# Four graph layers on one core: layer 1's weight factors transposed into other buffers with their bias sums behind that, and layer 3's statistics queued behind the head's kept values

## The chip, the core and the metric

The kernel runs on one core of a Trainium2 chip. The metric is the device time of one launch in microseconds (us), from the host's data in device memory to the result in device memory. Engines are named as in the profile: PE multiplies matrices (PEld is its loading of weights, which overlaps it), DVE and ACT work on vectors and read PE's results out of PSUM, POOL works on vectors in SBUF only, and SP issues most DMAs. Every engine runs its own queue of instructions in order, and waits on semaphores for the others.

## The reference

An input x of 128 graphs x 64 nodes x 512 features passes through four layers, each x = x + layer(relu(layernorm(x))), all in float32, with one adjacency matrix of 64 x 64 for each graph:

```python
h = maximum(layernorm(x), 0)
# layer 0: a gate from q, k and the adjacency, then a softmax over the 64 nodes
q, k = split(h @ Wqk);  w = mask * sum(q * (adj @ (k * mask)), -1) / sqrt(512)
x = x + softmax(w, axis=1)[:, :, None] * (h @ Wv)
# layer 1: attention whose exponentials are multiplied by adj
query, key, value = h @ Wq.T + bq, h @ Wk.T + bk, h @ Wv.T + bv
weight = adj * exp(query @ key.T);  x = x + (weight / sum(weight, 2)) @ value
# layer 2: attention with 8 heads, scores multiplied by 2 * adj, output projection
# layer 3: H = sum over k = 0..2 of (X_k @ Wk[k] + bk[k]), X_{k+1} = transition @ X_k,
#   with transition from adj * exp(leaky_relu(sj + si + ab)); x = x + relu(H)
```

In layer 1 the product query @ key.T needs Wq and Wk only as one folded matrix, and their biases bq and bk only as a column u, a row c and a number d.

## The kernel before

**Blocks and layers.** The 8192 tokens are cut into 32 blocks of 256 (two tiles of 128 tokens). Layers 0 and 1 alternate over pairs of blocks (`steps`), and write x to device memory; then layer 2 runs over the 32 blocks, then layer 3 (`layer3_step`).

**A product.** Each product of 256 tokens with a 512 x 512 weight is made with seven block products instead of eight (class `Product`): weights carry precomputed differences (`formed`, `chore`, in the places T1 to T4 of a weight slot), and the tokens carry four sums S made on POOL (`sums`). A product holds two PSUM banks, ab and dc. Its early block products (1, 6 into ab, 5, 4 into dc) are read by `keep_ab` (ACT copies a to p1, DVE adds b + p1 into u2, line 287) and `keep_dc` before the late ones (2, 7 into ab, 3 into dc) add to the same banks. `store` (lines 308 to 312) then writes the result with one copy on ACT, three additions on DVE and one on POOL. The pool `ps_mm` has four banks, so two products are under way at a time. `side_by_side` issues the early parts of two products, then their late parts, and calls the actions of `between` in between.

**Statistics.** `norm` makes the mean and variance of a block on DVE (lines 170 to 173), the power -1/2 on POOL (L175, rstd), a product on DVE (L177, nmr), and h on ACT (L185). `transposed` then turns h on PE (L196) into hT, copied by DVE and ACT.

**Weight factors.** For layers 0 and 1 the two factors q and k are loaded in a weight slot each (`factor`), transposed on PE (`transpose_weights`, L429), copied back over themselves (L435 on ACT, L437 on DVE), and multiplied (`folded`, L449) into the folded weight m. A slot has room for seven pieces of 512 columns; a factor takes four.

**Layer 1's set-up** (`setup1`) is a generator whose parts are issued by `next(setup)` between the parts of the work of layer 0: the loads; then five sums on DVE for d and u (`dots`, L487); then four more for c with a trip through device memory that spreads the row c1 over all partitions (L500, L502); then transposes, folding and the formed differences. Each of the sums multiplies 128 x 512 elements and adds them up; the bias lies in memory in the order (p k), and the factor is read in that order too, with a stride. The actions `further` call `next(setup)` twice during the first block of layer 0. Within `folded`, the end of block 0's softmax (`layer0_end`, its matmul sm_w at L406) is called after the first of four groups of matmuls.

**A layer 3 step** for block b makes y2 and y1 side by side (the head, `layer3_head`), then y0 (the tail). Between its early parts, `begin` makes the statistics and h of block b + 2; between early and late parts stands the end of block b - 1 (`layer3_end`: po on PE, tz on ACT at L934, an addition on POOL at L936, an addition into x on DVE at L937, the store). `layer3_dots` (L834) follows the tail.

**Order.** The instructions are put into the engines' queues by a planner (the tile framework's scheduler). It goes by data dependencies, by the program's order as a priority, and by when its own cost model believes an instruction to be ready; work from far down the program can be issued early. `tc.issue_after(ins)` says that what the block traces on the engine of `ins` is queued behind `ins`. It is an order of issue on that one engine, not a wait.

Of the kernel before, what the change touches and what calls it, by code (L numbers as in the profile page):

```python
# [8 lines left out]
FP = mybir.dt.float32  # L9
AF = mybir.ActivationFunctionType  # L10
ALU = mybir.AluOpType
AX = mybir.AxisListType

P = 128
N = 64
D = 512
K = D // P
# [8 lines left out]
def kernel(ctx: ExitStack, tc: tile.TileContext, a: dict, out: bass.AP):  # L26
# [7 lines left out]
    nc = tc.nc  # L34
# [4 lines left out]
    const = ctx.enter_context(tc.tile_pool(name="const", bufs=1))  # L39
    wpool = ctx.enter_context(tc.tile_pool(name="weights", bufs=1))  # L40
    big = ctx.enter_context(tc.tile_pool(name="big", bufs=2))
    med = ctx.enter_context(tc.tile_pool(name="med", bufs=3))
    snap = ctx.enter_context(tc.tile_pool(name="snap", bufs=2))
    small = ctx.enter_context(tc.tile_pool(name="small", bufs=3))
    ps_tr = ctx.enter_context(tc.tile_pool(name="ps_tr", bufs=2, space=bass.MemoryType.PSUM))
# [34 lines left out]
    def slot(place: int, name: str):  # L80
        return wpool.tile([P, 7, 2, F], FP, tag=f"w{place}", name=name)
# [3 lines left out]
    def formed(w, engine):  # L85
        for to, x, y in sums_of_weights:
            last = engine.tensor_tensor(w[:, to], w[:, x], w[:, y], ALU.subtract)  # L87
        return last
# [39 lines left out]

    def factor(ap, which: str, layer: int, queue):

        w = slot({"q": 4, "k": 5}[which], f"{which}_{layer}")
        w = w.rearrange("p s k o -> p (s k o)")[:, : K * D].rearrange("p (k o) -> p k o", k=K)
        for k in range(K):
            queue.dma_start(w[:, k, :], ap[k * P : (k + 1) * P, :])
        return w

    f0 = [
# [66 lines left out]
    def norm_T(x, name: str):  # L204
        hs = norm(x, name)
        return hs, transposed(hs, name)

    behind = [None]

    def sums(hT, name: str, places=("S", "S")):  # L210
# [18 lines left out]
    class Product:  # L229
# [52 lines left out]
        def keep_ab(self):  # L282


            self.p1, self.u2 = self.temp("p1"), self.temp("u2")
            nc.scalar.copy(self.p1, self.a)  # L286
            self.kept = nc.vector.tensor_tensor(self.u2, self.b, self.p1, ALU.add)  # L287

        def keep_dc(self, bias=None):

# [126 lines left out]
    def transpose_weights(*pairs):  # L417

        pts = [
            [  # L420
                pool.tile([P, K, P], FP, tag=tag, name=f"tw_{name}_{m}")
                for m, (pool, tag) in enumerate(places)
            ]
            for w, name, places, on_scalar in pairs
        ]
        for k in range(K):
            for (w, *_), mine in zip(pairs, pts):
                for m, pt in enumerate(mine):
                    nc.tensor.transpose(pt[:, k, :], w[:, k, m * P : (m + 1) * P], ident)  # L429
        last = [None, None]  # L430
        for m in range(K):
            for (w, _, _, on_scalar), mine in zip(pairs, pts):
                flat = mine[m].rearrange("p k i -> p (k i)")
                if m in on_scalar:
                    last[1] = nc.scalar.copy(w[:, m, :], flat)  # L435
                else:
                    last[0] = nc.vector.tensor_copy(w[:, m, :], flat)  # L437
        return last

    in_mm = ((ps_mm, "mm"),) * K  # L440
    elsewhere = ((ps_tr, "tr"), (ps_sc, "sc")) * 2

    def folded(aT, bT, layer: int, place: int, amid=lambda: None):

        m = slot(place, f"fold{layer}")
        for i in range(K):
            pm = ps_mm.tile([P, D], FP, tag="mm", name=f"pf_{layer}_{i}")
            for k in range(K):
                nc.tensor.matmul(  # L449
                    pm, aT[:, k, i * P : (i + 1) * P], bT[:, k, :],  # L450
                    start=(k == 0), stop=(k == K - 1),
                )
            nc.scalar.copy(m[:, quarters[i // 2][0], i % 2, :], pm[:, :F])
            nc.vector.tensor_copy(m[:, quarters[i // 2][1], i % 2, :], pm[:, F:])
            if i == 1 - layer:
                amid()
        return m

    def setup0():
        m = folded(*f0, 0, 0, lambda: turned(0))  # L460
        last = formed(m, nc.vector)

        msc = const.tile([P, n_tok // P], FP, tag="msc", name="msc")
        with tc.issue_after(behind_norm[0][1].ins):
            nc.vector.tensor_scalar(msc, mcol, -(float(D) ** -0.5), None, ALU.mult)
        return m, msc, last

    def setup1():


        qT, kT = (factor(a[f"L1_W{c}"], c, 1, nc.sync) for c in "qk")

        bias = big.tile([P, 2, P, K], FP, tag="v", name="b1qk")
        for i, n in enumerate(("L1_bq", "L1_bk")):
            nc.sync.dma_start(
                bias[:, i], a[n].rearrange("(o p) k -> o p k", o=1).to_broadcast([P, P, K])
            )
        w1v = fetched("L1_Wv", 3, nc.sync)
        yield
        u = const.tile([P, K], FP, tag="u1", name="u1")  # L480
        cc = small.tile([P, K], FP, tag="cc", name="c1", bufs=1)
        d = const.tile([P, 1], FP, tag="d1", name="d1")

        def dots(*sums):
            for to, x, by in sums:
                junk = med.tile([P, P, K], FP, tag="e2", name="bias1", bufs=3)
                nc.vector.scalar_tensor_tensor(  # L487
                    junk, x, 1.0, bias[:, by], ALU.mult, ALU.mult, accum_out=to
                )

        def columns(w):
            return [w[:, k, :].rearrange("q (k p) -> q p k", k=K) for k in range(K)]

        dots((d, bias[:, 0], 1))
        dots(*((u[:, k : k + 1], x, 1) for k, x in enumerate(columns(qT))))
        yield
        dots(*((cc[:, k : k + 1], x, 0) for k, x in enumerate(columns(kT))))

        crow = tc.dram_tile([1, D], FP, name="c1_row")
        nc.sync.dma_start(crow.rearrange("o (k p) -> p (o k)", p=P), cc)  # L500
        c1 = const.tile([P, 2, D + 1], FP, tag="u3", name="c1")[:, 0, :D]
        nc.sync.dma_start(c1, crow.to_broadcast([P, D]))  # L502
        yield
        transpose_weights((qT, "q1", in_mm, range(K)))
        transpose_weights((kT, "k1", elsewhere, (1, 3)))
        m = folded(kT, qT, 1, 2, lambda: layer0_end(0, *softmax))
        formed(m, nc.gpsimd)
        with tc.issue_after(behind[0].ins):
            formed(w1v, nc.gpsimd)
        w2 = [fetched(f"L2_W{c}", 4 + i, nc.sync) for i, c in enumerate("qk")]  # L510
        for w in w2:
            later(w)
        yield m, u, c1, d, w1v, w2
# [471 lines left out]
    def turned(i: int):  # L985
        layer, b = steps[i]
        normed[i] = normed[i], transposed(normed[i], f"{layer}_{b}")
# [19 lines left out]
    def turned2(b: int):  # L1007
# [1 line left out]
            normed2[b] = transposed(normed2[b], f"2_{b}")  # L1009

    taken = transpose_weights(
        (f0[0], "q0", in_mm, (2, 3)),
        (f0[1], "k0", ((ps_sc, "sc"), (ps_tr, "tr")) * 2, (0, 1)),
    )
    with tc.issue_after(taken[0].ins), tc.issue_after(taken[1].ins):
        prepare(0)
# [12 lines left out]
    for i, (layer, b) in enumerate(steps):  # L1029
        if i == len(steps) - 2:  # L1030
            fetch2(0)
        between = [[], [chore], []]
        if i == 0:
            for n in (1, 2):
                between[n].append(further)
        if i == 1:
            begun = []
            made1 = next(setup)
        for n, end in begun:
            between[n].append(end)  # L1040
        begun = []
        if i + 1 < len(steps):
            between[0].append(lambda: prepare(i + 1) if i else second())
            between[2].append(lambda: turned(i + 1))
        else:
            fetch2(1)
            between[0].append(lambda: first2(0, of_v))
            between[2].append(lambda: turned2(0))
        if layer == 0:
            softmax = layer0(b, *loaded[b], *normed[i], between, open_end if b % 2 else nothing)  # L1050
            begun = [(0, lambda b=b, softmax=softmax: layer0_end(b, *softmax))]
        else:
            of_v, *attention = layer1(
                b, *loaded[b], *normed[i], between, open_end if b % 2 else nothing
            )

            def open_end(b=b, a=attention):
                layer1_end(b, loaded[b][0], *a, x1[b])
                if b == n_blk - 2:
                    fetch2(2)  # L1060

        if i == len(steps) - 3:
            made2 = setup2()
# [2 lines left out]
    w3, made_in = {}, []  # L1066
    made3 = normed3 = None

    ending, behind_y0 = [lambda: None], [None]

    def layer3_step(b: int, ahead: bool = True):

# [6 lines left out]
        def begin():  # L1079
            nonlocal normed3  # L1080
            if b + 2 < n_blk and ahead:
                with tc.issue_after(behind_y0[0].ins):
                    normed3 = layer3_norm(b + 2)

        y = layer3_head(b, ops, [
            [begin], [ending.pop()], [lambda: next(stages, None), lambda: next(stages, None)]
        ])
        yield
        tail = layer3_tail(b, al, ops, y)
# [2 lines left out]
            yield  # L1092
        r, y0, kept = next(tail)
        ending.append(lambda: layer3_end(b, x, al, y, r, y0))
        behind_y0[0] = kept
        if b + 1 == n_blk:
            ending[0] = lambda: layer3_last(b, x, al, y, r, y0, ops, kept)
        if b + 2 < n_blk:
# [146 lines left out]
```

## Time and profile before

| | |
|---|---|
| Time before, median of 3 runs | 2640.34 us (2638.94 to 2640.64) |
| The profiled execution's own time | 2638.83 us |
| Span of the profiled execution, first to last instruction | 2637.0 us |
| Granted TensorE clock | 1.000 |
| Weight factors of layer 0, folding, first statistics | 0 to 26 us |
| Layer 0, block 0, and layer 1's set-up | 26 to 64 us |
| Layers 0 and 1, four steps for a pair of blocks | 59.7 us |
| Layer 2, one block | 28.63 us |
| Layer 3, one block, from b = 2 to b = 28 | 21.93 us |

The page gives the busy time of each engine, the chain of work that ended last, the costliest groups of instructions and the DMA issues. Line numbers (L257) are those of the kernel before. A line of a timeline reads: start, duration, engine, line, operation, output <- inputs, shapes, how many, and in brackets the idle time of the engine before it with what ended it. Equal instructions that follow each other are merged: x4 with 1.03 us is four of them from the first start to the last end. A matmul with a 4-byte type is recorded twice per call. A matmul's end is modelled, so what PE lost is read from the distance of starts. A line of waits reads: engine, what waited <- what it waited for, us in total, how often, and the longest.

### The profile page before, as it was taken

What the parts mean: (1) busy time and instruction counts of PE and PEld (TensorE: products, weight loads), DVE (VectorE), ACT (ScalarE), POOL (GpSimd) and SP (SyncE); (2) the same over time, 40 slices, a digit from 0 to 9 for tenths busy, and PEclk for the clock granted to TensorE, in tenths of its full rate; (3) what the DMA queues carried; (4) which work ended last, traced back from release to release, by engine and by line L of the source; (5) the groups of instructions that cost most, each with busy time, mean ns of one, the idle gap of its engine ahead of it and who ended that gap; (6) DMA issues with size and microseconds to landing.
All of it is one profiled execution on the core that took longest, in us unless ns stands there. A gap on an engine that the chain in (4) does not pass through costs nothing.

```text
span 2637.0 us, 52785 instructions
## 1 busy us (share of the span) xinstructions
PE 2618.7 (99%) x20752; PEld 2253.1 (85%) x20752; DVE 1701.5 (65%) x4400; ACT 939.9 (36%) x2292; POOL 1289.4 (49%) x1582
## 2 busy tenths in 40 slices
PE   8999999999999999999999999999999999999999
PEld 5888888888888889999999999999887777777777
DVE  5666666666666666566556656656666666666665
ACT  2343434333443343333333333333323333333332
POOL 2443343333334345656655655655565555555554
PEclk9999999999999999999999999999999999999999
DMA  5111111111111122111111111111211111111110
GB/s 162 62 40 35 35 35 36 35 46 41 38 48 35 35 67 79 45 45 40 45 46 40 37 53 37 39 53 38 74 51 52 52 52 51 52 52 52 51 51 33
DMA packets 103200, 129.81 MB, mean 49 GB/s; under 512 B 40870, under 2 KB 50086, under 8 KB 102952
## 3 DMA queue, kind: packets, MB, share of 16 engines
q1 hardware_dynamic: 102376, 125.38, 14.4%
q8 instruction: 164, 2.69, 0.4%
q10 hardware_dynamic: 576, 1.05, 0.1%
q14 instruction: 84, 0.69, 0.1%
HBM read 76.07 MB, written 50.34 MB: 48 GB/s over the span
## 4 chain that ended last, share of the span: by engine, by line
PE 95%; DVE 2%; DMA 1%; POOL 1%; ACT 0%; issue 0%; SPq 0%; POOLq 0%; ACTq 0%; DVEq 0%
PE ab_v L257 12%; PE ab_y L257 12%; PE dc_v L257 9%; PE dc_y L257 9%; PE ab_g L250 4%; PE ab_k L250 4%; PE ab_q L250 4%; PE tr L196 4%; PE ab_g L257 4%; PE ab_o L257 4%; PE dc_g L250 3%; PE po L398 3%; PE dc_g L257 3%; PE dc_k L250 3%; PE dc_q L250 3%; PE dc_o L257 3%
## 5 line engine op out<-in xcount | busy, mean ns | idle before, releaser
L175 POOL TENSOR_TENSOR rstd<-ve,neghalf 128x2 f32<-128x2 f32 x128 | 89.6, 700 | 445.2 <-DVE ve L173 445.1
L185 ACT ACTIVATE h<-x,nmr,rstd 128x512 f32<-128x512 f32 x256 | 194.4, 806 | 212.6 <-DVE nmr L177 212.6
L257 PE MATMUL ab_y<-L_Wk,hT 128*128 128x256 f32 x768 | 206.9, 392 | 0.6 <-DVE u_y L309 0.3
L257 PE MATMUL ab_v<-L_Wv,hT 128*128 128x256 f32 x768 | 200.9, 384 | 1.6 <-DVE u_v L287 0.9
L257 PEld LDWEIGHTS ab_y<-L_Wk,hT 128*128 128x128 f32 x768 | 135.7, 189 | 74.1 <-DVE r L896 23.5
L257 PE MATMUL dc_v<-L_Wv,S 128*128 128x256 f32 x768 | 197.3, 379 | 0.0
L257 PE MATMUL ab_y<-L_Wk,S 128*128 128x256 f32 x768 | 197.1, 379 | 0.0
L257 PE MATMUL ab_v<-L_Wv,S 128*128 128x256 f32 x768 | 197.1, 379 | 0.0
L257 PE MATMUL dc_y<-L_Wk,S 128*128 128x256 f32 x768 | 192.8, 380 | 0.0
L170 DVE BATCH_NORM_STATS2 stats<-x 128x6 f32<-128x512 f32 x256 | 164.9, 674 | 8.3 <-DMA x<-x 8.3
L257 PEld LDWEIGHTS dc_y<-L_Wk,S 128*128 128x128 f32 x768 | 145.6, 190 | 20.9 <-issue 0.8
L257 PEld LDWEIGHTS ab_y<-L_Wk,S 128*128 128x128 f32 x768 | 145.9, 190 | 19.8
L257 PEld LDWEIGHTS ab_v<-L_Wv,S 128*128 128x128 f32 x768 | 145.9, 190 | 19.8
L257 PEld LDWEIGHTS dc_v<-L_Wv,S 128*128 128x128 f32 x768 | 143.4, 190 | 18.9 <-POOL L_Wv L87 0.8
L257 PEld LDWEIGHTS ab_v<-L_Wv,hT 128*128 128x128 f32 x768 | 135.8, 190 | 17.6 <-DVE u_v L287 1.3
L936 POOL TENSOR_TENSOR tz<-tz,y 128x512 f32<-128x512 f32 x62 | 90.1, 1453 | 105.6 <-ACT tz L934 105.5
L196 PE MATMUL tr<-ident,h 128*128 128x128 f32 x1024 | 133.3, 273 | 0.0
L196 PEld LDWEIGHTS tr<-ident,h 128*128 128x128 f32 x1024 | 117.8, 141 | 7.7 <-issue 0.5
L222 POOL TENSOR_TENSOR S<-hT 128x256 f32<-128x256 f32 x128 | 100.6, 786 | 43.8 <-ACT hT L199 43.6
L225 POOL TENSOR_TENSOR S<-hT 128x256 f32<-128x256 f32 x128 | 106.9, 835 | 7.4 <-DVE hT L201 7.3
L223 POOL TENSOR_TENSOR S<-S,hT 128x256 f32<-128x256 f32 x128 | 101.9, 796 | 11.4 <-DVE ve L173 9.4
L286 ACT COPY p_y<-ab_y 128x256 f32<-128x256 f32 x96 | 35.1, 366 | 200.6 <-PE ab_y L257 192.0
(250 smaller groups left out, 6407.7 us busy)
## 6 DMA issues: line engine op xcount, KB each, us to landing
x<-x SPq DMA_DIRECT2D x128, 512.0 KB, 3.5
x<-in_x_dram SPq DMA_DIRECT2D x32, 512.0 KB, 3.5
out_dram<-x SPq DMA_DIRECT2D x31, 512.0 KB, 2.8
adjT<-in_adjT_dram SPq DMA_DIRECT2D x64, 64.0 KB, 2.0
adjq<-in_adj_dram SPq DMA_DIRECT2D x64, 64.0 KB, 2.3
L_Wk<-in_L_Wk_dram SPq DMA_DIRECT2D x16, 256.0 KB, 4.5
L_Wv<-in_L_Wv_dram SPq DMA_DIRECT2D x12, 256.0 KB, 5.2
q<-in_L_Wqk_dram ACTq DMA_DIRECT2D x4, 256.0 KB, 4.7
```

The source lines that it names most:

```text
L170: nc.vector.bn_stats(stats[:, t, :], x[:, t, :])
L175: by_rows = nc.gpsimd.tensor_tensor(rstd, ve, neghalf, ALU.pow)
L185: nc.scalar.activation(h, x[:, t, :], AF.Relu, bias=nmr[:, t : t + 1], scale=rstd[:, t : t + 1])
L196: nc.tensor.transpose(pt[:, k, :], h[:, k * P : (k + 1) * P], ident)
L222: nc.gpsimd.tensor_tensor(S1, A21, A22, ALU.add)
L223: nc.gpsimd.tensor_tensor(S2, S1, A11, ALU.subtract)
L225: behind[0] = nc.gpsimd.tensor_tensor(S3, A11, A21, ALU.subtract)
L250: nc.tensor.matmul(dst[:, m * P : (m + 1) * P], w[:, place, k, m * P : (m + 1) * P], left[:, k, :], start=key not in self.begun, stop=last ...
L257: nc.tensor.matmul(dst, left[:, k, :], w[:, place, k, :], start=key not in self.begun, stop=last and k == 1, skip_group_check=True,)
L286: nc.scalar.copy(self.p1, self.a)
L398: nc.tensor.matmul(ps[t][half[g ^ t]], e[half[g], t, :], us[t][half[g]], start=True, stop=True)
L936: nc.gpsimd.tensor_tensor(tz[t], tz[t], y0[:, t, :], ALU.add)
```

## The change

`factor` returns seven pieces of a slot, of which the first four are loaded. In layer 1 the transposed factors are written to the three free pieces of the own slot and to one place (T1 or T2) of the folded weight's slot, not over the loaded ones. The loaded ones stay, and so the nine bias sums are made after the transposing: on DVE behind the last copy of k, with the bias rows rearranged by two ACT copies beforehand, so that bias and factor are both read in a row. The end of block 0's softmax is put on PE behind the first group of folding matmuls. In layer 3 `begin` moves from the head's first place to its second and is queued on DVE behind the latest `keep_ab` sum, not behind the last addition of the preceding y0. The parts of it that matter:

```diff
     def factor(ap, which: str, layer: int, queue):
-        w = slot({"q": 4, "k": 5}[which], f"{which}_{layer}")
-        w = w.rearrange("p s k o -> p (s k o)")[:, : K * D].rearrange("p (k o) -> p k o", k=K)
+        w = slot({"q": 4, "k": 5}[which], f"{which}_{layer}").rearrange("p s k o -> p (s k o)")
+        w = [w[:, k * D : (k + 1) * D] for k in range(7)]
         for k in range(K):
-            queue.dma_start(w[:, k, :], ap[k * P : (k + 1) * P, :])
+            queue.dma_start(w[k], ap[k * P : (k + 1) * P, :])
         return w
...
             self.kept = nc.vector.tensor_tensor(self.u2, self.b, self.p1, ALU.add)
+            kept_ab[0] = self.kept
...
-            for (w, _, _, on_scalar), mine in zip(pairs, pts):
+            for (_, _, _, on_scalar, to), mine in zip(pairs, pts):
                 flat = mine[m].rearrange("p k i -> p (k i)")
                 if m in on_scalar:
-                    last[1] = nc.scalar.copy(w[:, m, :], flat)
+                    last[1] = nc.scalar.copy(to[m], flat)
                 else:
-                    last[0] = nc.vector.tensor_copy(w[:, m, :], flat)
+                    last[0] = nc.vector.tensor_copy(to[m], flat)
...
             if i == 1 - layer:
-                amid()
+                with tc.issue_after(last.ins):
+                    amid()
...
         w1v = fetched("L1_Wv", 3, nc.sync)
         yield
+
+        rows = [med.tile([P, K, P], FP, tag="pT", name=f"b1_{i}", bufs=3) for i in range(2)]
+        for i, r in enumerate(rows):
+            nc.scalar.copy(r.rearrange("o k p -> o p k"), bias[:, i])
+        rows = [r.rearrange("o k p -> o (k p)") for r in rows]
+        yield
...
-        dots((d, bias[:, 0], 1))
-        dots(*((u[:, k : k + 1], x, 1) for k, x in enumerate(columns(qT))))
-        yield
-        dots(*((cc[:, k : k + 1], x, 0) for k, x in enumerate(columns(kT))))
-
-        crow = tc.dram_tile([1, D], FP, name="c1_row")
-        nc.sync.dma_start(crow.rearrange("o (k p) -> p (o k)", p=P), cc)
         c1 = const.tile([P, 2, D + 1], FP, tag="u3", name="c1")[:, 0, :D]
-        nc.sync.dma_start(c1, crow.to_broadcast([P, D]))
-        yield
-        transpose_weights((qT, "q1", in_mm, range(K)))
-        transpose_weights((kT, "k1", elsewhere, (1, 3)))
-        m = folded(kT, qT, 1, 2, lambda: layer0_end(0, *softmax))
+        m = slot(2, "fold1")
+        qt, kt = (
+            f[K:] + [m[:, spare].rearrange("p k o -> p (k o)")]
+            for f, spare in ((qT, T1), (kT, T2))
+        )
+        transpose_weights((qT, "q1", in_mm, range(K), qt))
+        taken = transpose_weights((kT, "k1", elsewhere, (1, 3), kt))
+        folded(kt, qt, 1, m, lambda: layer0_end(0, *softmax))
         formed(m, nc.gpsimd)
         with tc.issue_after(behind[0].ins):
             formed(w1v, nc.gpsimd)
+
+        def dots(*sums):
+            for to, x, by in sums:
+                junk = med.tile([P, D], FP, tag="e2", name="bias1", bufs=3)
+                nc.vector.scalar_tensor_tensor(
+                    junk, x, 1.0, rows[by], ALU.mult, ALU.mult, accum_out=to
+                )
+
+        with tc.issue_after(taken[0].ins):
+            dots((d, rows[0], 1))
+            dots(*((u[:, k : k + 1], qT[k], 1) for k in range(K)))
+            dots(*((cc[:, k : k + 1], kT[k], 0) for k in range(K)))
+
+        crow = tc.dram_tile([1, D], FP, name="c1_row")
+        nc.sync.dma_start(crow.rearrange("o (k p) -> p (o k)", p=P), cc)
+        nc.sync.dma_start(c1, crow.to_broadcast([P, D]))
...
         if i == 0:
-            for n in (1, 2):
-                between[n].append(further)
+            between[1].append(further)
...
             if b + 2 < n_blk and ahead:
-                with tc.issue_after(behind_y0[0].ins):
+                with tc.issue_after(kept_ab[0].ins):
                     normed3 = layer3_norm(b + 2)
         y = layer3_head(b, ops, [
-            [begin], [ending.pop()], [lambda: next(stages, None), lambda: next(stages, None)]
+            [], [begin, ending.pop()], [lambda: next(stages, None), lambda: next(stages, None)]
         ])
```

Layer 0's factors are still transposed over themselves.

More of the change, by code (lines that the diff above doesn't have):

```diff
@@ L206, in norm_T @@
         return hs, transposed(hs, name)
+    kept_ab = [None]
     behind = [None]
@@ L423, in transpose_weights @@
             ]
-            for w, name, places, on_scalar in pairs
+            for w, name, places, on_scalar, to in pairs
         ]
@@ L428, in transpose_weights @@
                 for m, pt in enumerate(mine):
-                    nc.tensor.transpose(pt[:, k, :], w[:, k, m * P : (m + 1) * P], ident)
+                    nc.tensor.transpose(pt[:, k, :], w[k][:, m * P : (m + 1) * P], ident)
         last = [None, None]
         for m in range(K):
-            for (w, _, _, on_scalar), mine in zip(pairs, pts):
+            for (_, _, _, on_scalar, to), mine in zip(pairs, pts):
                 flat = mine[m].rearrange("p k i -> p (k i)")
                 if m in on_scalar:
-                    last[1] = nc.scalar.copy(w[:, m, :], flat)
+                    last[1] = nc.scalar.copy(to[m], flat)
                 else:
-                    last[0] = nc.vector.tensor_copy(w[:, m, :], flat)
+                    last[0] = nc.vector.tensor_copy(to[m], flat)
         return last
@@ L441, with folded @@
     elsewhere = ((ps_tr, "tr"), (ps_sc, "sc")) * 2
-    def folded(aT, bT, layer: int, place: int, amid=lambda: None):
-        m = slot(place, f"fold{layer}")
+    def folded(aT, bT, layer: int, m, amid=lambda: None):
         for i in range(K):
@@ L448, in folded @@
             for k in range(K):
-                nc.tensor.matmul(
-                    pm, aT[:, k, i * P : (i + 1) * P], bT[:, k, :],
+                last = nc.tensor.matmul(
+                    pm, aT[k][:, i * P : (i + 1) * P], bT[k],
                     start=(k == 0), stop=(k == K - 1),
@@ L455, in folded @@
             if i == 1 - layer:
-                amid()
+                with tc.issue_after(last.ins):
+                    amid()
         return m
     def setup0():
-        m = folded(*f0, 0, 0, lambda: turned(0))
+        m = folded(*f0, 0, slot(0, "fold0"), lambda: turned(0))
         last = formed(m, nc.vector)
@@ L482, in setup1 @@
         d = const.tile([P, 1], FP, tag="d1", name="d1")
[L484 to L492, printed above, removed]
-        dots((d, bias[:, 0], 1))
-        dots(*((u[:, k : k + 1], x, 1) for k, x in enumerate(columns(qT))))
-        yield
-        dots(*((cc[:, k : k + 1], x, 0) for k, x in enumerate(columns(kT))))
-        crow = tc.dram_tile([1, D], FP, name="c1_row")
-        nc.sync.dma_start(crow.rearrange("o (k p) -> p (o k)", p=P), cc)
-        c1 = const.tile([P, 2, D + 1], FP, tag="u3", name="c1")[:, 0, :D]
-        nc.sync.dma_start(c1, crow.to_broadcast([P, D]))
-        yield
-        transpose_weights((qT, "q1", in_mm, range(K)))
-        transpose_weights((kT, "k1", elsewhere, (1, 3)))
-        m = folded(kT, qT, 1, 2, lambda: layer0_end(0, *softmax))
+        c1 = const.tile([P, 2, D + 1], FP, tag="u3", name="c1")[:, 0, :D]
+        m = slot(2, "fold1")
[6 more added lines that the diff above has]
+        folded(kt, qt, 1, m, lambda: layer0_end(0, *softmax))
         formed(m, nc.gpsimd)
@@ L1011 @@
     taken = transpose_weights(
-        (f0[0], "q0", in_mm, (2, 3)),
-        (f0[1], "k0", ((ps_sc, "sc"), (ps_tr, "tr")) * 2, (0, 1)),
+        (f0[0], "q0", in_mm, (2, 3), f0[0]),
+        (f0[1], "k0", ((ps_sc, "sc"), (ps_tr, "tr")) * 2, (0, 1), f0[1]),
     )
@@ L1067 @@
     made3 = normed3 = None
-    ending, behind_y0 = [lambda: None], [None]
+    ending = [lambda: None]
     def layer3_step(b: int, ahead: bool = True):
@@ L1094, in layer3_step @@
         ending.append(lambda: layer3_end(b, x, al, y, r, y0))
-        behind_y0[0] = kept
         if b + 1 == n_blk:
```

## The prediction

> **What bounds it now.** The page first, for the busy shares; then the waits of PE, for what is left to win.
>
> ```profile
> PE 2618.7 (99%) x20752; PEld 2253.1 (85%) x20752; DVE 1701.5 (65%) x4400; ACT 939.9 (36%) x2292; POOL 1289.4 (49%) x1582
> ```
> ```profile
> PE ab_g L257 <- DVE u_g L287: 2.1, 1, 2.1
> PE sm_w L406 <- DVE wd L555: 1.0, 1, 1.0
> PE ab_v L257 <- DVE u_v L287: 0.9, 1, 0.9
> PE pf L449 <- DVE q L437: 0.6, 1, 0.6
> PE tw_q L429 <- DVE u_g L309: 0.6, 1, 0.6
> ```
>
> PE is the bound; only what it loses between matmuls can be won. Apart from 4.8 us for the first weights and a tail of 5.5 us (last matmul 2631.5, span 2637.0) these are among its longest waits. All but the fourth lie at 35 to 50 us, where layer 1 is set up. The timeline there:
>
> ```profile
> 33.49 1.03 PE L257 MATMUL dc_g<-fold,hT 128*128 128x256 f32 x4
> 33.87 1.04 DVE L487 SCALAR_TENSOR_TENSOR bias<-q,b1qk 128x512 f32<-128x512 f32 x1 [1.72 <-DMA q<-in_L_Wq_dram]
> 34.92 0.41 DVE L287 TENSOR_TENSOR u_v<-ab_v,p_v 128x256 f32<-128x256 f32 x1
> 35.39 1.13 PE L257 MATMUL ab_v<-L_Wv,hT 128*128 128x256 f32 x4 [0.87 <-DVE u_v L287]
> 40.79 0.41 DVE L287 TENSOR_TENSOR u_g<-ab_g,p_g 128x256 f32<-128x256 f32 x1
> 41.26 1.13 PE L257 MATMUL ab_g<-fold,hT 128*128 128x256 f32 x4 [2.14 <-DVE u_g L287]
> 47.00 1.91 PE L429 MATMUL tw_k<-ident,k 128*128 128x128 f32 x16
> 49.87 0.46 PE L406 MATMUL sm_w<-wd,ones_bd 128*128 128x128 f32 x2 [0.96 <-DVE wd L555]
> 50.38 1.13 PE L449 MATMUL pf<-q,k 128*128 128x512 f32 x2
> ```
>
> The small sums u_v and u_g, which release PE, stand in DVE's queue behind the bias sums (L487).
>
> Layer 3 hides a second loss. 27 steps take 21.93 us, but the step that makes no statistics (b = 30) takes 21.78. Two timelines, a step with and the step without:
>
> ```profile
> 2244.26 1.52 ACT L185 ACTIVATE h<-x,nmr,rstd 128x512 f32<-128x512 f32 x2 [3.40 <-DVE nmr L177]
> 2246.20 2.10 ACT L934 ACTIVATE tz<-po,r 128x512 f32<-128x512 f32 x3
> 2250.12 0.69 DVE L937 SCALAR_TENSOR_TENSOR x<-tz,x 128x512 f32<-128x512 f32 x1 [1.16 <-POOL tz L936]
> 2250.30 1.03 PE L257 MATMUL dc_y<-L_Wk,S 128*128 128x256 f32 x4
> 2250.73 0.42 DVE L309 TENSOR_TENSOR u_y<-ab_y,p_y 128x256 f32<-128x256 f32 x1
> 2251.21 1.13 PE L257 MATMUL ab_y<-L_Wk,hT 128*128 128x256 f32 x4
> 2252.18 1.03 PE L257 MATMUL ab_y<-L_Wk,S 128*128 128x256 f32 x4
> ```
> ```profile
> 2600.32 0.42 DVE L309 TENSOR_TENSOR u_y<-ab_y,p_y 128x256 f32<-128x256 f32 x1
> 2601.20 1.03 PE L257 MATMUL dc_y<-L_Wk,S 128*128 128x256 f32 x4
> 2602.07 1.03 PE L257 MATMUL ab_y<-L_Wk,hT 128*128 128x256 f32 x4
> ```
>
> A group of four matmuls costs 0.864. With statistics, y0's first group starts 0.91 after the one before it, 0.06 after L309's end (L309 frees its PSUM bank), and lasts 0.97: 0.15 lost. Without, it starts 0.87 after, and L309 had ended 1.33 earlier. The chain: statistics, rstd, nmr, h on ACT, tz behind h, POOL's add L936, L937, L309.
>
> **Setup, part by part.** From dc_g at 33.49 to pf at 50.38 are 16.89 us. PE's work in it: seven groups of four (6.05), 8 transposes at 0.109 (0.87), 32 weight transposes (3.49), sm_w (0.22): 10.63. So 6.26 are lost.
>
> *Nine sums behind the copies of k.* Without them u_v can run at about 31.5 (p_v ends 30.60, statistics of block 1 31.39) and is needed at 34.35. Those statistics give h about 2.5 us earlier than 37.5, and u_g follows p_g (ab_g ends 33.5) by 36, needed at 37.8. The stores that free the banks for tw_q are no longer held up either, except dc_g's: its adds L310 and L311 end some 0.9 after the last late group, but 12 of tw_q's 16 transposes (1.31) need other banks. I charge 0.2; 0 to 0.6.
>
> *Transposing into other buffers.* As many copies as before (q 4 on ACT, k 2 and 2), none free: pf still waits for them. The nearest row is layer 0's same sequence, transposes, copies, pf: "PE pf <- DVE q", 0.6, and 0.8 counted between starts. Charge 0.8. That wd comes earlier than the copies needs POOL's store of gv (0.73) before its four S sums; if it comes after them, agg and wd still end near 43.5, and k is transposed at about 44.
>
> *sm_w behind the first pf group*: the same 0.22, inside pf; its consumers (x, then layer 1's h at 56.65, transposed at 74.72) keep some 10 us.
>
> So 6.26 - 0.8 - 0.2 = 5.26; I take 5.1, ends 4.0 and 5.5.
>
> *What the sums cost where they go.* Contiguous they should take the 0.65 of the bias by bias row, not 1.04: nine, 6 us on DVE during pf (13.7 us), which uses DVE for 4 copies of 0.42 and layer 0's softmax. Done by about 54. Hidden by pf; behind them on DVE wait block 0's statistics (53.68 now), with 10 us to spare. SP: c_row's DMA moves from 43.17 to about 54, lands 8.0 later as now, then c1; its reader (L601, 86.94) becomes 82. Behind c1 on SP wait L2's first weights, from 59.4 to about 62.4; their first chore (L100) could stand in POOL's queue until 67, and the next POOL work there (L312) comes at 70. If that cover went, PE would lose what is over.
>
> *fold's T1 and T2 hold q's and k's last quarter*, so the first of POOL's four subtractions (58.96 now) waits for pf's end: four at 1.24 to about 65; first reader 78.18 - 5.1 = 73.
>
> *Two row copies on ACT*, writing successive elements 512 bytes apart; no row shows that. Bounds: 0.59 (ACT's contiguous copy, L199) and 1.06 (DVE reading with such a stride, L487). ACT is idle from 20.14 to 22.99 for both; nothing binds them to a place, see the rivals.
>
> **Layer 3.** The statistics (2 x 0.64, 2 x 0.17, 0.17), rstd 0.70, nmr 0.16 and h 1.52 are all moved, no DMA. They now follow y1's kept sum, which follows p_y (possible at 2243.0, ACT idle): kept 2243.7, ve 2245.5, rstd 2246.3, h from 2246.6. tz can start when po lands, 2244.9, instead of 2246.20, so L937 and L309 come earlier by up to 1.3. POOL's rstd may stand before an L936 (+0.7 of L309's 1.33 in hand), still early enough. h's next reader, the dots at 2259.93, has 11 us. So 27 x 0.153 = 4.1, and step 2, which loses 0.58 at the same place: 4.7; ends 0 and 4.7 here, and below nothing in a rival. Step 1's statistics wait for a DMA and stay.
>
> The Trainium skill, Perfetto Trace Analysis, section Optimization Strategy, says that a gap that repeats can mean too few buffers. This gap does wait for a PSUM bank, and the change adds none: by the rule alone layer 3 would bring 0 and the sum would be 5.1. The step without statistics has the same banks and no gap, so the row decides.
>
> **Sum.** 5.1 + 4.7 = 9.8; I take 9.7. Span 2637.0 - 9.7 = 2627.3; its own time 2638.83 becomes 2629.1. That execution was 1.5 below the median, 2640.34, so 2630.6.
>
> **Rivals.**
> 1. *Layer 3's wait stays* (h slips between the parts of tz, 1.5 us in front of the last, more than the 1.33 in hand). For: ACT's order is the planner's, and h and tz's last part are ready within half a microsecond. Against: then L309 is ready before L937 and may go first. Where the loss stays as it is, setup alone remains: 2640.3 - 5.1 = 2635.2. With all of h in front, L309 ends 1.52 - 1.33 + 0.06 = 0.25 late, a step loses 0.35 instead of 0.15, and 27 x 0.2 = 5.4 eats the setup: 2640.6.
> 2. *A wait in setup takes the removed one's place*: the row copies stand before block 0's h (15.67) and wait for b1qk, issued at 12.43 and 13.18 while neighbours land in 4.5 to 7 us. h at 20 to 22, the transposes at 18.48 lose 2.5 to 4.5: 2633 to 2635. Against: h is ready before they land.
> 3. *Slower*: in layer 3 rstd stands on POOL behind both tz additions, and ACT's h still in front of y2's copy (L308). Then L936 ends at 2248.6, rstd 2249.3, h 2249.5 to 2251.1, L308 2251.45, L309 2251.9: PE at 2251.95, not 2251.21, 0.74 a step. 27 x 0.74 = 20 less 5.1: 2655. It decides from 0.19 a step on, where it eats the setup's gain. Against: a planner that puts rstd so late sees h late too, and L308 first.
> 4. *It does not do what it says*: the statistics already come after y1's kept sum. Step 2242 denies it (statistics 2241.3, kept 2246.07).
>
> **Chances.** Forecast 0.68; rival 1, 0.12; rival 2, 0.10; rival 3, 0.09; rival 4, 0.01. A measurement of this kernel can tell about 0.2%, 5.3 us, from no change. Faster by more: forecast, a third of rival 1, two thirds of rival 2, 0.78; slower 0.09; within, 0.13. The range runs from 2629.0 (setup 5.5, layer 3 4.7, 1 us of spread between runs) to 2636.5 (rival 1's first case with setup at 4.0); beyond it lie the rest of rival 1 and rival 3.
>
> **What would show it.** Right: L487's successors after the k copies; no wait of ab_v or ab_g in 30 to 45; pf about 5 us earlier; layer 3's steps 21.78, L309 ended 0.5 us or more before y0's first group. Wrong: pf later than 46.5; steps of 21.9 or more; new PE waits on h, S or tr.

## The result, and the profile after

The changed kernel takes 2663.52 us, the median of 5 runs, beside 2639.22 us for the kernel before on the same chip: a ratio of 1.0092, 95% interval 1.0077 to 1.0106. It is 24.3 us slower. The profiled execution is the slowest of the five, 2664.91 us; its span is 2663.1 us, 26.1 longer than the span before.

The waits of PE first (engine, line and tile waited for; us in total, times, longest):

```profile
PE dc_y L258 <- DVE y L313: 13.2, 28, 0.7
...
PE tr L196 <- ACT h L185: 3.6, 1, 3.6
PE pf L450 <- ACT k L437: 1.2, 2, 0.6
```

u_v and u_g of the set-up are gone from the head of the list, as forecast. Two waits are new: one of 3.6 us for block 0's h, and one of about 0.46 us (once 0.75) in 28 of layer 3's steps. Three of the prediction's signs of being wrong are there: a new wait of PE for h, steps above 21.9, and pf later than 46.5.

**The start.** ScalarE's timeline of the changed kernel (start, duration, engine, line, operation; in brackets the idle time before and what ended it), then TensorE's:

```profile
19.19 1.94 ACT L485 COPY b<-b1qk 128x512 f32<-128x512 f32 x2 [7.23 <-DMA b1qk<-in_L_bq_dram]
20.94 1.50 ACT L185 ACTIVATE h<-x,nmr,rstd 128x512 f32<-128x512 f32 x2
```
```profile
21.79 1.97 PE L196 MATMUL tr<-ident,h 128*128 128x128 f32 x8 [3.62 <-ACT h L185]
23.55 9.16 PE L450 MATMUL pf<-k,q 128*128 128x512 f32 x16
...
51.13 2.38 PE L450 MATMUL pf<-q,k 128*128 128x512 f32 x5 [0.59 <-ACT k L437]
```

The two row copies stand in ScalarE's queue in front of block 0's h, which ran at 15.67 before. They wait for b1qk until 19.19, h starts at 20.94, and the transposes at 21.79 instead of 18.48. That is rival 2. What comes next was in no case of the prediction: the eight transposes take 1.97 us and sixteen matmuls of pf 9.16, where the same sixteen took 7.03 before. The windows view gives the reason (window, length, PE busy and matmuls, granted clock as a share of full speed, DMA share, GB/s):

```profile
22.00:24.00 2.00, 2.00 (x9) 0.50 1.08 346
...
28.00:30.00 2.00, 2.00 (x6) 1.00 0.24 45
```

At the end of the idle time the clock was 0.50, and it came back to 1.00 before 28. So the matmuls at 32 us, 26.32 before, start 6.32 late: 3.3 from the wait and 3.0 from the clock. From there to layer 1's pf the change wins what it was forecast to win: pf at 51.13 against 50.38 is only 0.75 late, so 5.57 us came back.

**Layer 3.** 27 steps take 22.82 us each (one of them 23.11), 21.93 before; the step without statistics is 21.78 in both. One step of the changed kernel:

```profile
2256.41 0.69 ACT L943 ACTIVATE tz<-po,r 128x512 f32<-128x512 f32 x1 [0.59 <-PE po L400]
...
2257.76 1.27 POOL L945 TENSOR_TENSOR tz<-tz,y 128x512 f32<-128x512 f32 x1
2257.83 1.22 DVE L177 SCALAR_TENSOR_TENSOR nmr<-mv,rstd 128x2 f32<-128x2 f32 x1 [0.81 <-POOL rstd L175]
...
2259.08 1.52 ACT L185 ACTIVATE h<-x,nmr,rstd 128x512 f32<-128x512 f32 x2 [1.99 <-DVE nmr L177]
...
2260.61 1.38 ACT L943 ACTIVATE tz<-po,r 64x512 f32<-64x512 f32 x2
...
2261.82 1.03 PE L258 MATMUL dc_y<-L_Wk,S 128*128 128x256 f32 x4
2262.02 0.37 ACT L310 COPY y<-ab_y 128x256 f32<-128x256 f32 x1
...
2262.42 0.42 DVE L311 TENSOR_TENSOR u_y<-ab_y,p_y 128x256 f32<-128x256 f32 x1 [2.46 <-ACT y L310]
...
2262.90 1.13 PE L258 MATMUL ab_y<-L_Wk,hT 128*128 128x256 f32 x4
...
2263.44 1.20 DVE L946 SCALAR_TENSOR_TENSOR x<-tz,x 128x512 f32<-128x512 f32 x1 [0.59 <-POOL tz L945]
...
2263.87 1.03 PE L258 MATMUL ab_y<-L_Wk,S 128*128 128x256 f32 x4
...
2264.90 0.41 DVE L313 TENSOR_TENSOR y<-dc_y,u_y 128x256 f32<-128x256 f32 x1
...
2265.36 1.13 PE L258 MATMUL dc_y<-L_Wk,S 128*128 128x256 f32 x4 [0.46 <-DVE y L313]
...
2266.33 1.03 PE L258 MATMUL dc_y<-L_Wk,hT 128*128 128x256 f32 x4
```

Read it from the top. tz's first part runs as soon as po lands. Then ScalarE idles for 1.99 us, since next in its queue is h, and h waits for nmr: an instruction on 128x2 numbers that takes 1.22 us here, ending with POOL's addition that started 0.07 before it (it takes 0.16 where POOL is quiet). Only at 2260.61, behind h, come tz's other two parts, 3.5 us after the first one ended. Everything behind is late: y2's copy L310, then u_y (L311), which releases y0's ab group; then L946, 1.20 us beside POOL's next work, in front of L312 and L313, which release the dc group. From dc_y at 2261.82 to the second ab group at 2263.87 are 2.05 us, where two groups need 1.73: 0.32 lost. From there to 2266.33 are 2.46: another 0.73. Together 1.05 on 21.78, which makes the 22.82 of a step. Against before it is 27 x 0.89 = 24.0.

### The profile page after: what moved, and what is told of

Its sections match the earlier page's. It is cut to its first block, busy times and chain, and to the rows that moved or that the text cites. A ratio compares the mean times of both kernels' runs of the same rounds, so it can differ in the third digit from the quotient of the medians.

```text
span 2663.1 us, 52838 instructions
## 1 busy us (share of the span) xinstructions
PE 2630.5 (99%) x20752; PEld 2251.0 (85%) x20752; DVE 1739.0 (65%) x4400; ACT 949.1 (36%) x2294; POOL 1287.8 (48%) x1582
## 3 DMA queue, kind: packets, MB, share of 16 engines
q10 hardware_dynamic: 576, 1.05, 0.1%
## 4 chain that ended last, share of the span: by engine, by line
PE 84%; DVE 6%; ACT 4%; POOL 3%; issue 2%; DMA 1%; ACTq 0%; POOLq 0%; DVEq 0%
PE ab_v L258 12%; PE dc_v L258 9%; PE ab_y L258 7%; PE dc_y L258 7%; PE ab_g L251 4%; PE ab_k L251 4%; PE ab_q L251 4%; PE ab_g L258 4%; PE ab_o L258 4%; PE dc_g L251 3%; PE tr L196 3%; PE dc_g L258 3%; PE dc_k L251 3%; PE dc_q L251 3%; PE dc_o L258 3%; PE po L400 2%
## 5 line engine op out<-in xcount | busy, mean ns | idle before, releaser
L223 POOL TENSOR_TENSOR S<-hT 128x256 f32<-128x256 f32 x128 | 113.5, 886 | 46.8 <-ACT hT L199 46.5
L177 DVE SCALAR_TENSOR_TENSOR nmr<-mv,rstd 128x2 f32<-128x2 f32 x128 | 59.6, 466 | 109.9 <-POOL rstd L175 109.9
L945 POOL TENSOR_TENSOR tz<-tz,y 128x512 f32<-128x512 f32 x62 | 79.4, 1280 | 104.9 <-ACT tz L943 101.3
```

The lines of the kernel that those rows point to most:

```text
L177: scaled = nc.vector.scalar_tensor_tensor(nmr, mv[:, :, 0], -1.0, rstd, ALU.mult, ALU.mult)
L223: nc.gpsimd.tensor_tensor(S1, A21, A22, ALU.add)
L945: nc.gpsimd.tensor_tensor(tz[t], tz[t], y0[:, t, :], ALU.add)
```

## The experiments

Theory A, formed from this trace: the two losses are separate. At the start it is the place of the row copies, in front of block 0's h; in layer 3 it is h between the parts of tz, late because nmr runs beside POOL. Twelve kernels follow, all timed against the kernel before.

### Each part alone

e2_stats_back is the changed kernel with layer 3's statistics back where they were; e3_stats_alone is the kernel before with only layer 3's edit made. The lines of e2, which e3's turn round:

```
-                with tc.issue_after(kept_ab[0].ins):
+                with tc.issue_after(behind_y0[0].ins):
-            [], [begin, ending.pop()], [lambda: ...
+            [begin], [ending.pop()], [lambda: ...
```

> The changed kernel with layer 3's edit undone: the statistics are made in their old place behind y0's kept sum; the set-up as changed. Theory A (the steps' 22.82 us come from the place of the statistics alone): steps back to 21.93 us, 27 x 0.89 = 24 us less, about 2639.5 us. Rival theory B (the set-up's new buffers shift what the planner does in layer 3): steps stay near 22.8 us, about 2663 us.

> The kernel before with layer 3's edit alone. Theory A: steps of 22.82 instead of 21.93 us, 2640.3 + 24 to 24.6 = about 2664.5 us. Rival theory B (it takes both parts to slow layer 3): steps near 21.8 to 21.9 us, 2636 to 2640 us.

Measured: e2 2637.29 us, ratio 0.9994 (0.9985 to 1.0004), steps of 21.93, some 2 us less than forecast; e3 2663.16 us, 1.0091 (1.0076 to 1.0106), steps of 22.8. Layer 3's edit by itself costs the whole 24 us, and the set-up has no share in it. Theory B falls.

e2's trace also bears on the clock. Its pf starts at 47.28, 3.85 earlier than the changed kernel's. The counterparts of the lines above:

```profile
20.63 1.36 PE L196 MATMUL tr<-ident,h 128*128 128x128 f32 x8 [2.08 <-ACT h L185]
```
```profile
22.00:24.00 2.00, 2.00 (x6) 1.00 1.11 329
```

b1qk landed 1.2 earlier here, PE idled 2.08 us, and the clock stayed at 1.00. In b3 below the same wait was 3.47 us, and the clock was 0.50 from 22 to 24. The Trainium skill, TensorE: Matmul & The Clock Gate, section "HAM oscillation — how this bites in real kernels", gives about 3.4 us of idle time as the point from which the clock falls. These three rows, 2.08 on one side, 3.47 and 3.62 on the other, agree. e3's timeline and window, with the old set-up, do not:

```profile
41.02 1.90 PE L258 MATMUL ab_g<-fold,hT 128*128 128x256 f32 x4 [2.15 <-DVE u_g L288]
```
```profile
42.00:44.00 2.00, 2.00 (x7) 0.50 0.06 0
```

The clock fell here after 2.15 us, and so it did in f5 below, behind the same wait of 2.15; in the kernel before, in f6 and in f7 the wait at this place is 2.14 or 2.15 as well, and the clock stayed at 1.00. So the length of one wait doesn't settle it, and 3.4 us is no safe bound; what else decides, no run here shows. At this place the low clock cost nothing by pf: from this ab_g to pf e3 takes 9.10 us and the kernel before 9.12, since PE waits for other engines in that stretch in both.

### The row copies

e1_rows_loaded (changed kernel) and e4_both (layer 3 as before) take the bias rows, laid out as rows in memory, straight into row order, with no copies on ScalarE:

```
-        bias = big.tile([P, 2, P, K], FP, tag="v", name="b1qk")
...
+        rows = [med.tile([P, D], FP, tag="pT", ...) for i in range(2)]
+        for r, n in zip(rows, ("L1_bq", "L1_bk")):
+            nc.sync.dma_start(r, a[n].to_broadcast([P, D]))
...
-            nc.scalar.copy(r.rearrange("o k p -> o p k"), bias[:, i])
```

> The changed kernel with one thing taken out: layer 1's bias rows come from memory already in row order, so ScalarE makes no row copies and nothing of block 0's start waits for b1qk; layer 3 as changed. Theory A (block 0's h stood behind the row copies, TensorE waited 3.6 us for it and then worked at a clock of 0.5 for about 7 us): the 6.3 us at 18 to 32 us come back, h at about 15.7, pa at about 26.3, and 2663.5 - 6.3 = 2657.2 us. Rival theory B (the clock of 0.5 at 21 to 28 us belongs to this stage, whoever waits): the wait goes, some 3.3 us, the slow clock stays, 2660. Both leave layer 3's steps at 22.82 us.

> The set-up's part alone, with the bias rows loaded in row order, layer 3 as before. Theory A (the set-up's gain of 5.57 us between pa and pf is real, and was eaten by the wait for the row copies): 2640.3 - 5.5 = about 2634.8 us, or some 1 less by what drifts back later. Rival theory B (the gain at 26 to 51 us comes only because that stretch starts later, when its data have long landed): 2639 to 2641 us, with TensorE waiting in 26 to 45 us for something that lands late.

Measured: e1 2664.6 us, 1.0097 (1.008 to 1.0113); e4 2640.05 us, 1.0003 (0.9993 to 1.0012). Both missed what theory A expected, and by the medians alone theory A would have been given up. The trace says otherwise: in e4 no wait for h, the clock at 1.00, pf at 44.11, 6.27 us earlier than before, and layer 1's first scores 6.07 earlier. The gain is lost after that: 14 of layer 1's long steps take 44.53 us instead of 44.08, 14 x 0.45 = 6.3. e1 shows the same.

e8_rows_behind_hT (layer 3 as before) keeps the copies and queues them on ScalarE behind block 0's last copy of hT:

```
+                behind_norm.setdefault(1, nc.scalar.copy(ht, pt))
...
+        with tc.issue_after(behind_norm[1].ins):
+            for i, r in enumerate(rows):
+                nc.scalar.copy(r.rearrange("o k p -> o p k"), bias[:, i])
```

> The set-up's part alone (layer 3 as before), with the two row copies queued on ScalarE behind block 0's last copy of hT, so that block 0's h doesn't wait for b1qk. Theory A (the wait for the row copies is the set-up's only own loss): no wait of tr for h at 18 to 22 us, pf of layer 1 at about 44.2 us (6.2 us earlier than before), and 2640 - 6 = 2634 us if layer 1's long steps stay at 44.08 us. Rival theory E (the 44.53 us steps of layer 1, seen with loaded rows, belong to every set-up that starts about 6 us earlier): 14 x 0.45 = 6.3 us are given back there, 2640 us.

Measured: 2634.03 us, 0.9979 (0.997 to 0.9989). No wait for h, pf at 44.88, layer 1's long steps at 44.08 but for one. Theory A holds for the set-up and theory E falls: the earlier start doesn't by itself bring the 44.53. The same instructions in the same order do both. Two lines of VectorE from a long step of e4, and the same two from e8 (the time of the step's first scores, 461.66 and 460.65, is to be taken off):

```profile
474.06 0.42 DVE L312 TENSOR_TENSOR gv<-dc_g,u_g 128x256 f32<-128x256 f32 x1 [0.46 <-PE tr L196]
...
475.33 1.05 DVE L551 SCALAR_TENSOR_TENSOR agg<-gv,msc,agg 128x512 f32<-128x512 f32 x1
```
```profile
472.69 0.42 DVE L312 TENSOR_TENSOR gv<-dc_g,u_g 128x256 f32<-128x256 f32 x1
...
474.04 0.74 DVE L558 SCALAR_TENSOR_TENSOR agg<-gv,msc,agg 128x512 f32<-128x512 f32 x1
```

In e4 L312 starts 0.36 later in the step (12.40 against 12.04), agg then starts behind POOL's first S addition instead of ahead of it and takes 1.05, not 0.74; at the end u_g releases PE 0.35 late. Why L312 starts late, with its semaphore served at the same time in both, no run here shows. POOL's addition L314 starts at 12.02 in both, just ahead of L312 in e8, and may be what holds it in e4; no run takes it away. It stays open.

### The bias sums

s1_sums_early is e8 with the nine contiguous sums moved back ahead of the transposes:

```
+        dots((d, rows[0], 1))
+        dots(*((u[:, k : k + 1], qT[k], 1) for k in range(K)))
+        dots(*((cc[:, k : k + 1], kT[k], 0) for k in range(K)))
         yield
...
-        with tc.issue_after(taken[0].ins):
-            dots(...)
```

> The set-up's part alone with the row copies behind hT (2634.0 us), and in it the nine bias sums, contiguous as changed, moved back ahead of the transposes, where VectorE meets them before u_v and u_g. Theory A (the sums in front of u_v and u_g were the set-up's cost before): TensorE waits again for u_v or u_g, 1 to 3 us between 30 and 45 us; the sums are shorter than before (0.65 against 1.04 us), so less than the 3.0 us of before is lost: 2635 to 2637 us. Rival theory F (the shorter, contiguous sums were what helped, not their place): no such waits, 2634 us.

Measured: 2644.1 us, 1.0016 (1.0007 to 1.0025), 10 us behind e8. TensorE:

```profile
35.75 1.13 PE L258 MATMUL ab_v<-L_Wv,hT 128*128 128x256 f32 x4 [1.30 <-DVE u_v L288]
...
48.29 2.81 PE L450 MATMUL pf<-q,k 128*128 128x512 f32 x6 [1.56 <-DVE k L439]
```

u_v stands again behind a sum that waits for q (34.59 to 35.28), and ran at 32.80 in e8. pf is 3.41 us later than e8's. That much is the price of the sums' place, and theory F falls. Theory A's time was missed all the same, by 7 us: most of the rest is layer 1's long steps, which are at 44.53 to 44.56 here too (14 x 0.46 = 6.4).

### Layer 3: what of it costs

Three variants of e3. f5_h_behind_tz queues the statistics' ScalarE work behind tz's last part:

```
+            last_tz[0] = nc.scalar.activation(tz[t][out_at], ...)
...
+                with tc.issue_after(kept_ab[0].ins), tc.issue_after(last_tz[0].ins):
...
+            [], [ending.pop(), begin], ...
```

f6_tz_on_dve gives tz's first addition to VectorE; f7_place_only puts VectorE's old queue (behind y0's kept sum) back at the new place:

```
+            (nc.gpsimd if t else nc.vector).tensor_tensor(tz[t], tz[t], y0[:, t, :], ALU.add)
```
```
-                with tc.issue_after(kept_ab[0].ins):
+                with tc.issue_after(behind_y0[0].ins):
```

> The kernel before with layer 3's edit alone, and in it one thing changed: the statistics are built behind the ending of the block before and queued on ScalarE behind the last part of tz, so that h no longer stands between tz's parts. VectorE's queue is as the edit has it (statistics behind y1's kept sum). Theory A (the step's 1.05 us of loss is h, 1.52 us, in front of tz's last part): no loss, steps of 21.78 us, 27 x 1.04 = 28 us less than the edit alone (2663.2), about 2635 us. Rival theory B (the loss comes from VectorE's queue: the statistics and nmr, held up by POOL, stand in front of L946, and L946 in front of L312 and L313, whatever ScalarE does): steps stay at 22.4 us or more, 2652 us or more.

> The kernel before with layer 3's edit alone, and in it tz's first addition of y0 on VectorE instead of POOL, so that POOL's addition (1.27 us) does not run beside nmr. Theory A (nmr's 1.22 us beside POOL's addition, against 0.16 us alone, makes h about 1.06 us late, and that is the step's loss): nmr at 0.16 us, h earlier by 1.06 us, steps at 21.8 us, about 2635 us. Rival theory C (nmr's delay is not what decides; h ahead of tz's last part alone is): steps lose 1.52 us - 1.33 us in hand + 0.06 = 0.25 us or more, 22.0 to 22.8 us, 2642 to 2663 us.

> The kernel before with layer 3's statistics built at the new place in the program (behind y1's kept values, next to the ending), but queued on VectorE as before, behind y0's kept sum of the block before. Theory A (the queue, not the place, sends the statistics behind y1's kept sum and h behind po): statistics run as before, h ends before po lands or little after, steps at 21.8 to 21.93 us, 2636 to 2640 us. Rival theory D (the place decides the order): steps at 22.8 us, 2663 us.

Measured: f5 2635.01 us, 0.9984 (0.9974 to 0.9993), and f6 2634.89 us, 0.9983 (0.9973 to 0.9992), both with 27 steps of 21.78; f7 2641.32 us, 1.0008 (0.9998 to 1.0017), steps of 22.00. A step of f5:

```profile
2265.67 2.09 ACT L937 ACTIVATE tz<-po,r 128x512 f32<-128x512 f32 x3 [0.59 <-PE po L400]
...
2267.09 1.22 DVE L177 SCALAR_TENSOR_TENSOR nmr<-mv,rstd 128x2 f32<-128x2 f32 x1 [0.81 <-POOL rstd L175]
...
2268.34 1.52 ACT L185 ACTIVATE h<-x,nmr,rstd 128x512 f32<-128x512 f32 x2 [0.58 <-DVE nmr L177]
```

nmr still takes 1.22 us and VectorE still has L942 (after's L946) ahead of L312 and L313, but tz is done first, and nothing is lost. Theory B falls. A step of f6:

```profile
2265.45 0.16 DVE L177 SCALAR_TENSOR_TENSOR nmr<-mv,rstd 128x2 f32<-128x2 f32 x1
...
2265.65 1.52 ACT L185 ACTIVATE h<-x,nmr,rstd 128x512 f32<-128x512 f32 x2 [0.22 <-DVE nmr L177]
```

Here h does stand before tz's last part, but tz has two parts ahead of it, nmr takes 0.16, and ScalarE idles 0.22 for it instead of 1.99. Nothing is lost either, so h ahead of tz's last part is not a loss by itself, and theory C falls. That the loss needs ScalarE's wait for a late nmr as well is argued, not shown: f6 also moves one part of tz ahead of h and adds 0.70 us of VectorE work, so the share of nmr alone isn't separated by it. In f7 the statistics come before y1's kept sum again; h's second part falls between y1's two kept copies, and a step loses 0.07 more than before. Theory D's 22.8 falls; theory A's 21.93 was a little too good.

### Both parts, mended

b1_rows_tz_dve is e8's and f6's edit on the changed kernel, b2_rows_h_behind e8's and f5's, b3_tz_dve_only f6's alone.

> Both parts of the change, each mended: the row copies queued behind block 0's last copy of hT, and tz's first addition on VectorE. If the two gains add up (set-up 2639.4 - 2634.0 = 5.4 us, layer 3 2639.4 - 2634.9 = 4.5 us), about 2629.5 us, with layer 3's steps at 21.78 us and layer 1's long steps at 44.08 us but for one. Rival theory E: the earlier start puts layer 1's or layer 3's steps into a slower pattern, as loaded rows did (44.53 us), 2634 to 2636 us.

> Both parts of the change, each mended: the row copies queued behind block 0's last copy of hT, and layer 3's h queued on ScalarE behind the last part of tz. If the two gains add up (5.4 and 2639.4 - 2635.0 = 4.4 us), about 2629.6 us with steps of 21.78 us. Rival theory E: a slower pattern in layer 1 or layer 3, 2634 to 2636 us.

> The changed kernel with tz's first addition on VectorE and nothing else: the row copies stay in front of block 0's h. Theory A (layer 3's loss and the row copies' wait are independent): 28 us less than the changed kernel, 2663.5 - 28 = about 2635 us if TensorE's clock falls to 0.5 after the wait, 2632.5 us if it doesn't (the changed kernel with layer 3 as before took 2637.3 us and showed no fall). The wait of tr for h at 18 to 22 us stays, 2 to 3.6 us.

Measured: b1 2629.27 us, 0.9959 (0.9946 to 0.9971); b2 2629.66 us, 0.996 (0.9946 to 0.9973); b3 2634.42 us, 0.9978 (0.9969 to 0.9987), each against 2640.14 for the kernel before. The gains add up: pf at 44.17 in b1, layer 1's long steps at 44.08 but for one, layer 3's at 21.78. b1 and b2 can't be told apart; they beat the kernel before by 10.9 and 10.5 us, and so the changed one, 24.3 behind it, by some 35. In b3 the wait for h was 3.47 us, with the clock at 0.50 after it: the 5.15 us between b3 and b1 are what the row copies' place costs. The low clock's share varies: from the transposes to pa b3 takes 9.55 us and the changed kernel 10.85, where the kernel before takes 7.84, so 1.7 and 3.0.

## Why the prediction was wrong

**What bounds it, and the set-up's sum: right.** Layer 1's set-up won 5.57 us between 26 and 51 us (5.1 taken, 4.0 to 5.5 given, so just above the upper end). pf waits 0.59 for k's copies (0.8 charged), tw_q has no wait for a store (0.2 charged), the moved sums cost nothing and their old place 3.4 us (s1). e8 brings 2639.4 - 2634.03 = 5.4.

**The row copies: size at its upper bound, place wrong.** The two take 1.94 us from the first start to the last end, and one by itself 1.06 or 1.07, where 0.59 to 1.06 was given. The step that failed is "ACT is idle from 20.14 to 22.99 for both; nothing binds them to a place". Idle time on an engine is no claim on a place in its queue: nothing bound them, and so they could stand ahead of h as well. Rival 2 named this, its counterargument ("h is ready before they land") did not hold, and it was priced at 2.5 to 4.5. The wait was 3.3, and the other 3.0 of the 6.32 came from a term that was in no sum of the prediction: the half clock after 3.6 us of idle time.

**Layer 3: the loss and its cause were read rightly, the way out was not.** The 0.153 a step is real and can be won: f5 and f6 have 21.78 (4.7 forecast; 4.4 and 4.5 measured). The step that failed is "h from 2246.6. tz can start when po lands": tz's start did come at po's landing, but h came in between its parts. By that working h starts 1.7 after po's landing; it started 2.67 after tz's first part did. The difference of 1.0 is nmr's: 0.16 in the row used, and 1.22 beside POOL's addition. The Trainium skill, SBUF — State Buffer, section "Who interferes with whom", says that a VectorE instruction with two inputs in SBUF contends with a POOL instruction that reads SBUF, that the shared ports are an exclusive lock, and that the order of issue decides who waits. This trace agrees: nmr reads mv and rstd, started 0.07 after POOL's addition and ended 0.02 after it; in f6, with that addition taken from POOL, nmr is at 0.16. The prediction weighed POOL's queue, not POOL's company.

**Rival 1 had the place and a wrong price.** It put h's 1.52 in front of tz's last part, less 1.33 in hand: 0.35 a step. But h at the head of the queue also holds ScalarE while it waits: 1.99 idle + 1.52 = 3.51 between tz's parts. Rival 3 had the consequence, y2's copy behind h and the end a loss of 0.74 a step (0.89 measured), with a wrong cause, rstd behind both tz additions: rstd stood ahead of both, and h was late all the same, so the argument against this rival, which spoke of a late rstd, missed the case that came.

**The sum.** Of the span's +26.1, layer 3's steps are 24.0 where a gain of 4.7 was forecast, the set-up 0.75 where 5.1 was; some 1.3 lie elsewhere, 0.46 of it in layer 1's first long step (44.54) and 0.29 in the one step of 23.11. With the two orders mended (b1) the forecast's own terms, 5.1 and 4.7, came out as 10.9 together.

## What to carry to other kernels

Work moved to an engine's idle time needs a place in that engine's queue as well: ask what it waits for, and who is queued behind it while it waits, and price the wait, not only the work. A short instruction on VectorE can take as long as the POOL instruction that runs beside it, so a moved step is priced with its new neighbours. When a part is mended and the time doesn't move, compare the steps of every stage before giving up the theory: e4's 6 us had been won at 44 us and lost again by 1000.

## What the runs showed of the hardware

TensorE's clock went to 0.50 after idle times of 3.47 (b3) and 3.62 us (the changed kernel), but also after 2.15 us (e3, f5); it stayed at 1.00 after 2.08 (e2) and after 2.14 to 2.15 (the kernel before, f6, f7). It cost 3.0 us on top of the wait in the changed kernel, 1.7 in b3 and nothing in e3. VectorE's nmr takes 1.22 us instead of 0.16 beside a POOL addition of 1.27, and x's update 1.20 instead of 0.69. One and the same order of instructions in layer 1 ran at 44.08 or at 44.53 us a step, for 14 steps in a row; up to VectorE's L312, where the two part, the traces of e4 and e8 show no difference of more than 0.03 us, but for one POOL product (am) 0.1 us apart, 6 us ahead of that.
